# The closing exponential in a tile of its own, and the opening of the feed-forward part shared out anew

## The chip, the cores and the metric

The kernel runs on one core of a Trainium2 chip. The metric is the device time of one execution in microseconds (us); three executions gave 2990.84, 2991.1 and 2994.2 us, median 2991.1. A core has five engines that work through instruction queues of their own, in order: TensorE (PE in the profile; its weight loads are PEld), VectorE (DVE), ScalarE (ACT), GpSimd (POOL) and SyncE (SP), which here only issues DMAs. Engines wait for each other through semaphores.

## The reference

4096 nodes with 256 features and a 4096 x 4096 adjacency matrix go through two layers. Each layer adds a graph part and a feed-forward part to the running x:

```python
x = x + gnn0(layernorm(x), adj)     # 4 heads of 64, softmax over the neighbours, elu
x = x + ffn0(layernorm(x))          # 30 times: h + .01 tanh(h); h*sigmoid(h); layernorm; h @ W.T + b
x = x + gnn1(layernorm(x), adj)     # two graph layers, one after the other
x = x + ffn1(layernorm(x))          # router, the best 2 of 6 experts
```

A graph layer computes, for each head, scores `leaky_relu(f1[i] + f2[j])` where there is an edge, a softmax over j, the weighted sum of the values and `elu` of the result. So there are three graph layers in all: g0, g1 and g2.

## The kernel before, in words

Rows are taken in tiles of 128 and groups of four tiles (512 rows; 8 groups). The kernel has six stages in order: graph layer g0, the feed-forward part of 30 steps, g1, g2, and the experts (routing and products).

**A graph layer** (`attention`) begins with a prologue that multiplies the rows by the weights (`columns` transposes a group and writes the tile xT, L276; `products` multiplies, L302). Its main loop has 128 units, in the order of chunk c (8 row tiles, 4 chunks), head h (4) and column block q (8). In a unit ScalarE or VectorE makes signs (L461, L459), VectorE masks them (L569, L575), and TensorE adds up products in the PSUM tiles acc (L521). The exponentials are split so that no exponential is needed per edge. The queues of VectorE and ScalarE are in the order of the code here (`manual_schedule`).

When the 8 units of a head are through, it is closed while the next head's first units run. `lower_sums` (ScalarE, L468) and `whole_sums` (VectorE, L472) take acc out into the tile u, which frees acc for the next head. Then `close` takes one step a unit: scale (L482), add (L486), add and reciprocal (L489, L491), divide (L495), exponential on ScalarE (L499), and `finish` (L625 or L627, then L628), which makes elu of it and adds the old x. `finish` ends with the store to DRAM (L629, on SP's queue). There is one buffer for u, and the exponential e is written into a free half of it:

```python
e = u[:, :, 1, :D]
nc.scalar.activation(e[:, :nt], o[:, :nt], AF.Exp)
```

L628 writes its result over e, so the store reads u. Adjacency masks come from DRAM in pieces of 1 MB (`load_mask`, L192) in g1 and g2, four for each chunk, during the chunk's last head before; they go through SP's queue too. The last head of a layer is closed after the loop (L603 to L608), outside the written order: a planner merges its steps among the instructions of the next stage by its own estimate of times.

Memory is given out in pools, stacked in the order in which they are opened and freed as a stack. The prologue's pools (prep, pw) and the closing pool (end) of a layer start at the same address, since the one pair is freed before the other is opened.

**The feed-forward part** works on units, one group in one step: 240 units. A unit passes through a pipeline over slots (`slot`): slot `at` does tanh of unit `at` on ScalarE (L881) and adds it to the input on GpSimd (L882); Silu (L869) and its f16 copy (L871) of unit at-2 on ScalarE, the rest of that split (L872) and the statistics (L896, L898) on VectorE, and a transposing DMA (L876, SP); the transposes of unit at-3 on TensorE (L845), their copy on ScalarE (L903), the standard deviation (L906 to L908); the matmuls of unit at-4 (L920, L923); and the scaling of unit at-5 (L853). The queues of TensorE, VectorE, ScalarE and GpSimd are in written order in this part. A manual dependency makes GpSimd's sum of unit `at` wait for L872 of unit at-2; in the very first slot it waits for `closed[0]`, the division L495 of the last close.

Its input must be normalised first, group by group: `measure` (VectorE, 4 x L748 and 4 x L750), `rate` (one small instruction on ScalarE, L756, three on GpSimd, L757 to L760), `init` (four ScalarE instructions, L766). Groups 0 to 3 are loaded into the tile ring and measured beside the last units of g0, by a table `side` that is keyed by units left (L788); groups 4 to 7 are handled in the first slots (L909 to L914). Groups 6 and 7 hold the rows of g0's last chunk, so their loads (L822) wait for the store of the last close.

The weights of the three graph layers (`weights`, L128) lie in the pool keep from the start of the kernel, though those of g2 are only loaded during g1 (L977).

Of the kernel before, what the change touches and what calls it, by code (L numbers as in the profile page):

```python
# [11 lines left out]
F32 = mybir.dt.float32  # L12
# [5 lines left out]
AF = mybir.ActivationFunctionType  # L18
# [28 lines left out]
def gnn_ffn_kernel(ctx: ExitStack, tc: tile.TileContext, a: dict, out: bass.AP):  # L47
# [79 lines left out]

    def weights(tag, W, a_src, a_dst, norm):  # L128


        w = keep.tile([P, KC, C + 2 * H], F32, name=f"{tag}_w")

# [28 lines left out]
    def attention(tag, src, norm, w, front, chunks, first, ends, following, side={}):  # L161
# [7 lines left out]
        with ExitStack() as scope:  # L169
# [306 lines left out]
            def close(c, h, u):  # L476

                nt, t0 = chunks[c], starts[c]
                begin, finish = ends
                more = begin(t0, nt, h, end)  # L480
                v = u[:, :, 0, :]
                nc.vector.tensor_tensor(  # L482
                    v[:, :nt], v[:, :nt], r[:, t0 : t0 + nt, h : h + 1].to_broadcast([P, nt, DV]), OP.mult
                )
                yield
                nc.vector.tensor_tensor(v[:, :nt], v[:, :nt], u[:, :nt, 1, :], OP.add)  # L486
                yield

                nc.vector.tensor_tensor(v[:, :nt], v[:, :nt], hs[:, :, h, :].to_broadcast([P, nt, DV]), OP.add)  # L489
                z = end.tile([P, CM, 1], F32, name="z", bufs=2)  # L490
                nc.vector.reciprocal(z[:, :nt], v[:, :nt, D : D + 1])  # L491
                yield
                o = v[:, :, :D]
                closed[:] = [
                    nc.vector.tensor_tensor(o[:, :nt], v[:, :nt, :D], z[:, :nt].to_broadcast([P, nt, D]), OP.mult)  # L495
                ]
                yield
                e = u[:, :, 1, :D]
                nc.scalar.activation(e[:, :nt], o[:, :nt], AF.Exp)  # L499
                yield  # L500
                finish(t0, nt, h, o[:, :nt], e[:, :nt], more)
                yield
# [107 lines left out]
    def to_rows(dst, src=None):  # L610
# [12 lines left out]
        def finish(t, n, h, u, e, old):  # L623
            if src is None:
                nc.vector.tensor_scalar(u, u, 0.0, -1.0, op0=OP.max, op1=OP.add)  # L625
            else:
                nc.vector.scalar_tensor_tensor(u, u, 0.0, old, op0=OP.max, op1=OP.add)  # L627
            nc.vector.scalar_tensor_tensor(e, e, 1.0, u, op0=OP.min, op1=OP.add)  # L628
            nc.sync.dma_start(block(dst, t, n, h), e)  # L629

        return begin, finish


    layers = [weights("g0", a["L0_gnn_W"], a["L0_gnn_a1"], a["L0_gnn_a2"], True)]
    for n in range(2):
        av = a[f"L1_gnn_a{n + 1}"]
        layers.append(weights(f"g{n + 1}", a[f"L1_gnn_W{n + 1}"], av[:, :D], av[:, D:], not n))
    gw = [w for w, _ in layers]
    w0 = gw[0]

# [121 lines left out]

    def init(g):
        rs, nm = rates.pop(g)
        for r in range(G):
            nc.scalar.activation(  # L766
                x1[g][:, r, :], x1[g][:, r, :], AF.Identity, scale=rs[:, r : r + 1], bias=nm[:, r : r + 1]
            )

# [5 lines left out]
    def front(prep, small_ps):  # L775
# [17 lines left out]
        20: [(load, 3)],  # L793
        14: [(measure, 0)],
        8: [(measure, 1)],
        4: [(rate, 0), (rate, 1), (measure, 2)],
        1: [(measure, 3), (init, 0), (init, 1), (rate, 2), (rate, 3)],
# [14 lines left out]
    with ExitStack() as scope:  # L812
# [18 lines left out]
        th, zs, mvs, rs, zT, zT16, pos = {}, {}, {}, {}, {}, {}, {}  # L831
        units = FFN_STEPS * NG
        def slot(at):
            g, part = divmod(at - 4 * NG, 3 * NG)
# [32 lines left out]
            if 0 <= u < units:  # L867
                z = zs[u] = work.tile([P, G, C], F32, name="z")
                nc.scalar.activation(z, th.pop(u), AF.Silu, scale=0.01)  # L869
                z16 = work.tile([P, 2, G, P], F16, name="z16", bufs=4)  # L870
# [6 lines left out]
            if at < units:  # L877
# [3 lines left out]
                nc.scalar.activation(th[at], was, AF.Tanh, scale=0.01)  # L881
                ins = nc.gpsimd.tensor_tensor(th[at], th[at], was, OP.add)  # L882
                if not at:
                    lower = closed[0]
                if lower is not None:
                    tc.add_manual_dep(
                        ins.ins,
                        lower.ins.name,
                        mybir.DependencyInfo(mybir.DependencyClass.Sync, mybir.DependencyReason.DATA),
                        reason="the port that both use",  # L890
                    )
            if 0 <= u < units:
# [8 lines left out]
            if 0 <= u < units:  # L901
# [6 lines left out]
                nc.gpsimd.tensor_tensor(rs[u], rs[u], under[:, int(u >= units - NG), :], OP.mult)  # L908
            if 4 <= at + 3 < NG:  # L909
                rate(at + 3)  # L910
            if 2 <= at + 2 < NG:
                init(at + 2)
            if 4 <= at + 4 < NG:
                measure(at + 4)  # L914
            u = at - 4
# [19 lines left out]
        with tc.manual_schedule(  # L935
# [5 lines left out]
            }  # L941
        ):
            for at in range(units):
                slot(at)
# [25 lines left out]


    def centre_weights(prep, small_ps):
        layers[1][1][2](small_ps)
# [5 lines left out]
    for n in range(2):  # L979
# [3 lines left out]
            not n,  # L983
            gw[n + 1],
            None if n else centre_weights,
# [463 lines left out]
```

## Time and profile before

One execution was profiled. Engines' busy times are of that one.

| | |
|---|---|
| median of three runs | 2991.1 us |
| the profiled execution | 2996.19 us |
| its span, first to last instruction | 2994.5 us |
| granted TensorE clock, mean | 0.975 |
| busy: TensorE, VectorE, ScalarE, GpSimd | 2805.8, 2735.7, 2472.4, 1160.0 us |
| g0's last matmul ends | about 602.3 us |
| first, last tanh of the feed-forward part (start) | 602.9, 1547.0 us |
| g1's last, g2's first large matmul | about 2116.9, 2128.1 us |
| g2's last sums begin (L472) | 2674.0 us |

In a line of groups the columns are: line, engine, operation, written tile <- read tiles, shapes, count; busy us and mean ns of one; then the engine's idle us just before and what ended most of it. In a timeline line they are: start, duration, engine, line, operation, tiles, shapes, count, and in brackets the idle time before it with what ended it. SPq is SP's queue of DMA issues.

### The profile page before, as it was taken

What the parts mean: (1) busy time and instruction counts of PE and PEld (TensorE: products, weight loads), DVE (VectorE), ACT (ScalarE), POOL (GpSimd) and SP (SyncE); (2) the same over time, 40 slices, a digit from 0 to 9 for tenths busy, and PEclk for the clock granted to TensorE, in tenths of its full rate; (3) what the DMA queues carried; (4) which work ended last, traced back from release to release, by engine and by line L of the source; (5) the groups of instructions that cost most, each with busy time, mean ns of one, the idle gap of its engine ahead of it and who ended that gap; (6) DMA issues with size and microseconds to landing.
All of it is one profiled execution on the core that took longest, in us unless ns stands there. A gap on an engine that the chain in (4) does not pass through costs nothing. (4 is left out here: it accounts for less than half of the span.)

```text
span 2994.5 us, 82658 instructions
## 1 busy us (share of the span) xinstructions
PE 2805.8 (94%) x33923; PEld 2567.1 (86%) x33923; DVE 2735.7 (91%) x5756; ACT 2472.4 (83%) x3137; POOL 1160.0 (39%) x1085
## 2 busy tenths in 40 slices
PE   7899999979999999999998999999789999986996
PEld 6799999958888888888887999999689999985996
DVE  7999999989999999999998899999689989986775
ACT  6799999888888888888877999999689989963342
POOL 3000000089999999999982000000200000014663
PEclk9999999989999999999999999999999999997998
DMA  9998785053333333433352122120302132123253
GB/s 287 276 255 249 221 245 144 23 127 69 69 70 68 68 68 68 68 68 68 69 119 101 31 93 85 36 90 24 107 22 91 52 106 79 52 85 137 80 172 136
DMA packets 484451, 320.08 MB, mean 107 GB/s; under 512 B 416589, under 2 KB 445418, under 8 KB 477930
## 3 DMA queue, kind: packets, MB, share of 16 engines
q1 hardware_dynamic: 474034, 290.27, 37.2%
q0 software_dynamic: 7104, 19.41, 2.0%
q8 instruction: 268, 4.39, 0.6%
q10 hardware_dynamic: 2936, 5.11, 0.5%
q14 instruction: 109, 0.89, 0.1%
HBM read 183.00 MB, written 52.04 MB: 78 GB/s over the span
## 5 line engine op out<-in xcount | busy, mean ns | idle before, releaser
L521 PE MATMUL acc<-vals,st 128*128 128x130 f16 x12288 | 1435.2, 219 | 44.5 <-DVE u L472 37.2
L521 PE MATMUL acc<-vals,below 128*128 128x130 f16 x12288 | 1434.9, 221 | 12.0 <-DVE below L575 11.4
L461 ACT ACTIVATE st<-f1b,nf 128x1024 int8<-128x1024 f32 x1265 | 1335.7, 1142 | 38.0 <-PE acc L521 24.0
L521 PEld LDWEIGHTS <-below 128*128 128x128 fp8e4 x12288 | 1178.0, 96 | 58.8 <-issue 53.4
L521 PEld LDWEIGHTS <-st 128*128 128x128 fp8e4 x12288 | 1209.5, 98 | 8.9 <-DVE st L569 6.9
L920 PE MATMUL po<-wT,zT 128*128 128x256 f32 x1920 | 575.0, 381 | 3.7 <-ACT zT L903 3.7
L923 PE MATMUL po<-w,zT 128*128 128x256 f16 x3840 | 577.0, 273 | 1.3 <-DMA zT<-z 1.3
L882 POOL TENSOR_TENSOR th<-th,y 128x1024 f32<-128x1024 f32 x232 | 548.5, 2364 | 14.8 <-issue 0.2
L923 PEld LDWEIGHTS <-zT 128*128 128x128 f16 x3840 | 376.0, 98 | 161.8 <-DMA zT<-z 2.0
L575 DVE TENSOR_TENSOR below<-m,st 128x1024 int32<-128x1024 int32 x384 | 470.0, 1224 | 32.9 <-DVE st L569 1.4
L569 DVE TENSOR_TENSOR st<-st,m 128x1024 int32<-128x1024 int32 x384 | 467.3, 1217 | 0.2
L853 DVE SCALAR_TENSOR_TENSOR y<-po,z_rs,bias 128x256 f32<-128x256 f32 x928 | 384.6, 477 | 1.7 <-PE tp L845 0.4
L896 DVE BATCH_NORM_STATS2 z_st<-z 128x6 f32<-128x256 f32 x960 | 335.9, 413 | 0.0
L920 PEld LDWEIGHTS po<-wT,zT 128*128 128x128 f32 x1920 | 290.6, 191 | 12.8 <-ACT zT L903 4.5
L869 ACT ACTIVATE z<-th 128x1024 f32<-128x1024 f32 x240 | 251.8, 1049 | 14.6 <-POOL th L882 14.4
L106 POOL TENSOR_TENSOR ln_rstd<-ln_rstd,mhalf 128x4 f32<-128x4 f32 x24 | 31.1, 1296 | 583.9 <-ACT acc L1102 497.9
L907 POOL TENSOR_TENSOR z_rs<-z_rs,mhalf 128x4 f32<-128x4 f32 x240 | 244.5, 1019 | 3.1 <-ACT z_rs L906 3.1
L881 ACT ACTIVATE th<-y 128x1024 f32<-128x1024 f32 x232 | 241.7, 1042 | 0.0
L903 ACT COPY zT<-tp 128x512 f32<-128x512 f32 x240 | 140.4, 585 | 91.8 <-PE tp L845 90.4
L459 DVE TENSOR_SCALAR st<-f1b,nf 128x1024 int8<-128x1024 f32 x271 | 201.2, 743 | 8.1 <-PE acc L521 8.1
L757 POOL TENSOR_TENSOR x_rs<-x_rs,mhalf 128x4 f32<-128x4 f32 x8 | 10.2, 1280 | 505.4 <-ACT x_rs L756 505.4
L436 POOL MEMSET hs<- 128x4 f32 x3 | 0.3, 102 | 494.5 <-DVE u L489 494.5
(260 smaller groups left out, 3142.3 us busy)
## 6 DMA issues: line engine op xcount, KB each, us to landing
ring<-in_adj_dram SPq DMA_DIRECT2D x64, 1024.0 KB
m<-edges SPq DMA_DIRECT2D x32, 1024.0 KB
f1b<-fd SPq DMA_DIRECT2D x48, 512.0 KB
edges<-m SPq DMA_DIRECT2D x16, 1024.0 KB
y<-yd SPq DMA_DIRECT2D x16, 512.0 KB
ew<-in_L_ffn_expert_w_dram SPq DMA_DIRECT2D x18, 256.0 KB
t<-in_x_dram SPq DMA_DIRECT2D x8, 512.0 KB
old<-in_x_dram SPq DMA_DIRECT2D x16, 256.0 KB
```

The lines of the kernel that those rows point to most:

```text
L461: nc.scalar.activation(out, f1, AF.Sign, bias=f2, scale=-1.0)
L521: nc.tensor.matmul(acc[:, i, cols], masked[part][:, at_i // TR, s, rows], v[:, cols], start=(j == 0 and part == 0), stop=(j == NT - 1 and ...
L569: nc.vector.tensor_tensor(above, above, whole, OP.bitwise_and)
L575: nc.vector.tensor_tensor(below, whole, above, OP.bitwise_xor)
L853: nc.vector.scalar_tensor_tensor(t[:, r, :] if end else y[:, g * G + r, :], po[:, r, :], rstd[:, r : r + 1], t[:, r, :] if end else bias, ...
L869: nc.scalar.activation(z, th.pop(u), AF.Silu, scale=0.01)
L881: nc.scalar.activation(th[at], was, AF.Tanh, scale=0.01)
L882: ins = nc.gpsimd.tensor_tensor(th[at], th[at], was, OP.add)
L896: nc.vector.bn_stats(st[:, r, :], z[:, r, :])
L907: nc.gpsimd.tensor_tensor(rs[u], rs[u], mhalf, OP.pow)
L920: nc.tensor.matmul(po[:, r, :], src[:, r * P : (r + 1) * P], wT, start=True, stop=False)
L923: nc.tensor.matmul(po[:, r, :], src16[:, part * G + r, :], w16[:, other, :], start=False, stop=(part == 1 and other == 1),)
```

## The change

It has five parts.

1. In `close`, e is a tile of its own in the pool end (2048 bytes a partition, one buffer). `closed` now holds two instructions of the last close: what `finish` returns (its last VectorE instruction, L628 of before), and the exponential.
2. To make room, g2's weights move from keep to a pool "late" that is opened after the feed-forward part.
3. The first sum of the feed-forward part (unit 0) is VectorE's; GpSimd's first is unit 1, and it waits for `closed[0]`, now the end of the close.
4. Groups 3, 4 and 5 are initialised by VectorE (one `tensor_scalar` a tile, after `closed[0]`). What the first slots do for groups 2 to 7 is a table, `opening`: groups 4 and 5 are measured ahead of slot 0, both their rates are in slot 1, the measuring of groups 6 and 7 moves from slots 2 and 3 to 3 and 4, and the rest by one or two slots. In `side`, measuring 0 and 1 move from 14 and 8 units before the end to 18 and 14, the rates of both from 4 to 10.
5. The first Silu waits for the close's exponential.

```diff
-    def weights(tag, W, a_src, a_dst, norm):
+    def weights(tag, W, a_src, a_dst, pool):
-        w = keep.tile([P, KC, C + 2 * H], F32, name=f"{tag}_w")
+        w = pool.tile([P, KC, C + 2 * H], F32, name=f"{tag}_w")
...
-                closed[:] = [
-                    nc.vector.tensor_tensor(o[:, :nt], v[:, :nt, :D], z[:, :nt].to_broadcast([P, nt, D]), OP.mult)
-                ]
+                nc.vector.tensor_tensor(o[:, :nt], v[:, :nt, :D], z[:, :nt].to_broadcast([P, nt, D]), OP.mult)
                 yield
-                e = u[:, :, 1, :D]
-                nc.scalar.activation(e[:, :nt], o[:, :nt], AF.Exp)
+                e = end.tile([P, CM, D], F32, name="e")
+                powers = nc.scalar.activation(e[:, :nt], o[:, :nt], AF.Exp)
                 yield
-                finish(t0, nt, h, o[:, :nt], e[:, :nt], more)
+                closed[:] = [finish(t0, nt, h, o[:, :nt], e[:, :nt], more), powers]
...
-            nc.vector.scalar_tensor_tensor(e, e, 1.0, u, op0=OP.min, op1=OP.add)
+            made = nc.vector.scalar_tensor_tensor(e, e, 1.0, u, op0=OP.min, op1=OP.add)
             nc.sync.dma_start(block(dst, t, n, h), e)
+            return made
...
+    def follows(ins, other, reason):
+        tc.add_manual_dep(
+            ins.ins,
+            other.ins.name,
+            mybir.DependencyInfo(mybir.DependencyClass.Sync, mybir.DependencyReason.DATA),
+            reason=reason,
+        )
-    def init(g):
+    def init(g, apart=False):
         rs, nm = rates.pop(g)
         for r in range(G):
-            nc.scalar.activation(
-                x1[g][:, r, :], x1[g][:, r, :], AF.Identity, scale=rs[:, r : r + 1], bias=nm[:, r : r + 1]
-            )
+            t = x1[g][:, r, :]
+            if apart:
+                ins = nc.vector.tensor_scalar(t, t, rs[:, r : r + 1], nm[:, r : r + 1], op0=OP.mult, op1=OP.add)
+                follows(ins, closed[0], "first the rows that others wait for")
+            else:
+                nc.scalar.activation(t, t, AF.Identity, scale=rs[:, r : r + 1], bias=nm[:, r : r + 1])
...
-        14: [(measure, 0)],
-        8: [(measure, 1)],
-        4: [(rate, 0), (rate, 1), (measure, 2)],
+        18: [(measure, 0)],
+        14: [(measure, 1)],
+        10: [(rate, 0), (rate, 1)],
+        4: [(measure, 2)],
...
+        opening = {
+            0: [(init, 2)],
+            1: [(rate, 4), (rate, 5), (init, 3, True)],
+            2: [(init, 4, True)],
+            3: [(init, 5, True), (measure, 6)],
+            4: [(rate, 6), (measure, 7)],
+            5: [(init, 6), (rate, 7)],
+            6: [(init, 7)],
+        }
...
-                nc.scalar.activation(z, th.pop(u), AF.Silu, scale=0.01)
+                ins = nc.scalar.activation(z, th.pop(u), AF.Silu, scale=0.01)
+                if not u:
+                    follows(ins, closed[1], "one change of tables")
...
-                ins = nc.gpsimd.tensor_tensor(th[at], th[at], was, OP.add)
-                if not at:
+                ins = (nc.gpsimd if at else nc.vector).tensor_tensor(th[at], th[at], was, OP.add)
+                if at == 1:
                     lower = closed[0]
...
-            if 4 <= at + 3 < NG:
-                rate(at + 3)
-            if 2 <= at + 2 < NG:
-                init(at + 2)
-            if 4 <= at + 4 < NG:
-                measure(at + 4)
+            for f, g, *how in opening.get(at, []):
+                f(g, *how)
...
+            measure(4)
+            measure(5)
             for at in range(units):
                 slot(at)
...
+    layer(2, ctx.enter_context(tc.tile_pool(name="late", bufs=1)))
```

More of the change, by code (lines that the diff above doesn't have):

```diff
@@ L627, in finish, with layer @@
                 nc.vector.scalar_tensor_tensor(u, u, 0.0, old, op0=OP.max, op1=OP.add)
-            nc.vector.scalar_tensor_tensor(e, e, 1.0, u, op0=OP.min, op1=OP.add)
+            made = nc.vector.scalar_tensor_tensor(e, e, 1.0, u, op0=OP.min, op1=OP.add)
             nc.sync.dma_start(block(dst, t, n, h), e)
+            return made
         return begin, finish
[L634 to L639, printed above, removed]
+    layers = [weights("g0", a["L0_gnn_W"], a["L0_gnn_a1"], a["L0_gnn_a2"], keep)]
+    w0 = layers[0][0]
+    def layer(n, pool):
+        av = a[f"L1_gnn_a{n}"]
+        layers.append(weights(f"g{n}", a[f"L1_gnn_W{n}"], av[:, :D], av[:, D:], pool))
+    layer(1, keep)
     def begin_weights(n):
@@ L881, in slot @@
                 nc.scalar.activation(th[at], was, AF.Tanh, scale=0.01)
-                ins = nc.gpsimd.tensor_tensor(th[at], th[at], was, OP.add)
-                if not at:
+                ins = (nc.gpsimd if at else nc.vector).tensor_tensor(th[at], th[at], was, OP.add)
+                if at == 1:
                     lower = closed[0]
                 if lower is not None:
[L886 to L891, printed above, removed]
+                    follows(ins, lower, "the port that both use")
             if 0 <= u < units:
@@ L983, in gnn_ffn_kernel @@
             not n,
-            gw[n + 1],
+            layers[n + 1][0],
             None if n else centre_weights,
```

## The prediction

> **What bounds the kernel now.** I read the page first: TensorE and VectorE are both busy for over nine tenths, so what matters is where TensorE stands still.
>
> ```profile
> span 2994.5 us, 82658 instructions
> PE 2805.8 (94%) x33923; PEld 2567.1 (86%) x33923; DVE 2735.7 (91%) x5756; ACT 2472.4 (83%) x3137; POOL 1160.0 (39%) x1085
> L521 PE MATMUL acc<-vals,st 128*128 128x130 f16 x12288 | 1435.2, 219 | 44.5 <-DVE u L472 37.2
> ```
>
> 37.2 of the 44.5 us that the attention's matmuls idle end with L472, the first step of a head's close: it empties the accumulators. The VectorE groups, with shapes kept apart, say what L472 itself waits for:
>
> ```profile
> L472 DVE TENSOR_TENSOR u<-acc,lo 128x520 f32<-128x520 f32 x96 | 66.9, 697 | 54.4 <-ACT lo L468 35.2 <-DMA h1d<-u 10.9 <-DMA x3d<-u 6.2
> ```
>
> 17.1 us are waits for the *store of the head before*, which reads u, the tile that L472 overwrites; its line's own view adds 1.7 us for x1d. The timelines (VectorE, then SP's queue, then TensorE) at the worst place, in the second graph layer:
>
> ```profile
> 2422.94 0.69 DVE L628 SCALAR_TENSOR_TENSOR u<-u 128x512 f32<-128x512 f32 x1
> 2430.71 0.70 DVE L472 TENSOR_TENSOR u<-acc,lo 128x520 f32<-128x520 f32 x1 [3.28 <-DMA x3d<-u]
> ...
> 2422.33 0.32 SPq L192 DMA_DIRECT2D m<-edges  x1
> 2423.66 0.46 SPq L629 DMA_DIRECT2D x3d<-u  x1
> ...
> 2431.46 0.27 PE L521 MATMUL acc<-vals,st 128*128 128x130 f16 x1 [2.39 <-DVE u L472]
> ```
>
> The store follows a 1 MB mask load and needs 7 us; all engines then stand. The same views between the two graph layers:
>
> ```profile
> 2127.40 0.60 ACT L276 ACTIVATE xT<-tp 128x512 f32<-128x512 f32 x1 [5.34 <-DMA h1d<-u]
> ...
> 2123.28 0.37 SPq L629 DMA_DIRECT2D h1d<-u  x1
> ...
> 2128.14 6.85 PE L302 MATMUL ph<-g_w,xT 128*128 128x264 f32 x16 [8.77 <-ACT xT L276]
> ```
>
> The next layer's xT lies in u's memory, so ScalarE waits for the last store. Last, the opening of the feed-forward part (ScalarE, VectorE, GpSimd, TensorE):
>
> ```profile
> 608.02 2.06 ACT L766 ACTIVATE ring<-ring,x_nm,x_rs 128x256 f32<-128x256 f32 x4
> 610.09 1.28 ACT L869 ACT_TABLE_LOAD   x1
> 611.39 1.06 ACT L869 ACTIVATE z<-th 128x1024 f32<-128x1024 f32 x1
> 616.82 1.04 ACT L869 ACTIVATE z<-th 128x1024 f32<-128x1024 f32 x1
> ...
> 608.15 2.42 DVE L627 SCALAR_TENSOR_TENSOR u<-u,old 128x512 f32<-128x512 f32 x1 [0.70 <-ACT u L499]
> 610.60 2.72 DVE L628 SCALAR_TENSOR_TENSOR u<-u 128x512 f32<-128x512 f32 x1
> ...
> 607.67 5.10 POOL L882 TENSOR_TENSOR th<-th,ring 128x1024 f32<-128x1024 f32 x2 [5.68 <-DVE u L495]
> ...
> 612.50 1.11 PE L845 MATMUL tp<-ident,z 128*128 128x128 f32 x4 [10.18 <-ACT z L869]
> ```
>
> TensorE is idle for 10.18 us and again for 4.30; ScalarE carries row groups (2.06 us each, L766) between the Silus, and the last close's L627 and L628 take 2.42 and 2.72 us beside GpSimd's sums. From 642.3 us TensorE runs without a gap, 3.92 us a unit; only what it starts earlier there counts.
>
> **The Trainium skill.** "SBUF — State Buffer", section "Who interferes with whom": a VectorE operation with two SBUF inputs and a GpSimd operation that reads SBUF exclude each other for a whole instruction. The trace agrees: 2.42 and 2.72 us there, 0.69 where GpSimd is idle. "DMA: Bandwidth & Descriptors", section "Latency and other measured facts": latency at HBM is 0.2 us, but 2 us under high load. Agrees in kind: stores landed after 2.8 us (613.35 to the load freed at 616.19), 4.1, 5.5 and 7 us, the longest behind mask loads. "ScalarE: Activation LUTs", section "What ACT_TABLE_LOAD costs": 1283 ns, and 1380 more for a drain; the trace shows the first and no gap for the second, so I use 1.3.
>
> **Part 1, the exponential's own tile.** The store reads e, so u is free once VectorE itself has read it (L628, in order before L472). The new wait sits on the next Exp, which overwrites e five units after L472: 19 us later, against a store of 7, so nothing. What the stalls cost TensorE I take from the cadence of L468, the ScalarE copy that starts with the end of a head's matmuls. Undisturbed: 29.97 to 30.0 us. After the closes with a store wait: 30.89, 29.97, 30.72 in layer one; 30.38, 33.53 (2427.26 to 2460.80), 30.79 in layer two. Over 29.98: 0.91+0+0.74+0.40+3.55+0.81 = **6.4 us**. Masks do not become late next: the one needed at such a close was loaded six units before. The fourth wait of layer one (5.49 us at 2116.54) gives nothing: the second L472 waits there for L468, which ends at 2117.49 anyway.
>
> In layer zero 1.11 and 0.57 us of VectorE idling end with x1d. VectorE is the bound there (572 of 600 us busy), so most of it comes back: **1.5** (0 to 1.7).
>
> Between the graph layers: prep and work pools of a layer start where the attention's closing pool starts. By the sizes in the code u is bytes 0 to 4160, two lo to 8320, z to 8384, and the new e 8384 to 10432. The next layer's small tiles and first xT (2272 to 6368) lie under u and lo, the second xT (6368 to 10464) under e. So the first xT waits for L628 (2123.25), not the landing (2127.40): **4.1 us**. The second xT, at 2136.15 before, moves to about 2132, after the landing. If e were laid first, this would be 0.
>
> **Part 2, the opening.** I walk the in-order queues with the trace's durations; walked in the old order, they start the f16 part of unit 4's matmuls at 643.25, where the trace has 643.21. New: L495 ends at 607.44 as before. The first sum runs on VectorE, priced by L370 (same shape, 1.22 us), while Exp runs; L627 and L628 take 0.69 each and end at 610.0 (before 613.3). ScalarE has no third group between Exp and the table load: Silu 0 at 609.4 (611.39). VectorE's groups 3 to 5 wait for L628 on their own queue, which costs nothing; L872 of unit 0 is behind group 3, but its port is taken until 612.5 anyway. GpSimd's first sum, unit 1, waits for L628 instead of following L495; behind it queue the rates of groups 4 and 5 (1.56 each). It runs 610.1 to 612.5, Silu 1 at 612.5 (616.82). Then the gain shrinks: the sum of unit 2 queues behind both rates, Silu 2 at 618.0 (624.00); group 6's measuring on VectorE comes after two groups of 4 x 0.325 and the Silus' statistics (1.6 us a unit), so rate 6 on ScalarE, ahead of Silu 3, holds that to 623.4 (630.21); group 6's initialisation on ScalarE waits for its rate, behind unit 4's sum on GpSimd, so Silu 4 is at 631.4 (635.49). Unit 4's matmuls get to the same point at 640.4, 2.8 earlier.
>
> The two unknowns: how VectorE's tensor_scalar behaves beside GpSimd (L1092, same shape, mean 452 ns with GpSimd near, 1.38 us for four without; if it waits out each sum, gain 1.95), and whether the planner puts the first sum before L482 (0.8 less). Together **2.3 us**, ends 1.2 and 2.85. ScalarE is relieved of 3 x 2.06 = 6.2 us; were all of it on the path, that is the upper bound. One change of tables stays one: the old order has only one there; its new wait (Silu 0 behind Exp) is met at 608.1, and what queues behind Silu 0 on ScalarE is late only if Exp is.
>
> SP's queue: the store of the last close is issued at 610.1 instead of 613.35, so the two loads behind it (L822) and unit 0's transposing DMA behind them come some 3 us earlier; the walk has that. Ring reloads behind the first sum wait for VectorE's instead, about 1 us earlier.
>
> **Part 3, nothing.** Measuring 1 (1.6 us) moves off the close at 571.88, where TensorE idled 2.31, but measuring 0 moves ahead of the close at 539.43; VectorE has no idle between, so the loss only changes place. If VectorE had cover at 532, this would gain 1.6. The moved measurings and rates issue no DMA; earlier rates use idle GpSimd. Layer two's weights swap one place in memory for another; nobody waits for them.
>
> **Sum.** 6.4 + 1.5 + 4.1 + 2.3 = 14.3. Profiled: 2994.5 to 2980.2 span. That execution took 2996.19 us, 5 over the median 2991.1; I apply the sum to the median: **2977**. A measurement can tell about 0.2%, 6 us.
>
> **Rivals.** (a) Half of it: xT is not freed (the layout differs) or the opening gives nothing since its rates queue behind the sums: 2980 to 2983. For: the walk already loses most of the 6.2 us. Against: the sizes above. (b) The opening gives all 6.2 and the measuring 1.6: 2991.1 - 6.4 - 1.5 - 4.1 - 6.2 - 1.6 = 2971. Against: GpSimd's rates. (c) Store waits belong to the profiled run, and stores land earlier without it: then 6.4+1.5+4.1 shrink to perhaps 3 and it ends at 2986 to 2990, no change. For: that run is 5 us longer. Against: 1 MB mask loads ahead of the stores are no matter of profiling. (d) Slower: a unit is 3.92 us on TensorE while VectorE is busy 19.97 of 20 us in steady units and GpSimd 19.2. If the new phase of VectorE against GpSimd makes L872 meet a running sum in each of some 235 units, the unit grows; from 0.06 us a unit it eats all 14.3, at 0.1 the time is 2991.1 - 14.3 + 23.5 = 3000. Against: each sum waits for L872 two units back, which restores the old phase.
>
> **Numbers.** My case 55%, (a) 20%, (b) 8%, (c) 10%, (d) 7%. My case alone: 2973 to 2981. Range with (a) and (b): 2971 to 2986. Faster by over 0.2% are mine, (a), (b): 0.83; same 0.10; slower 0.07.
>
> **What would show it.** L472 with no DMA among its releasers; heads of 30.0 us throughout both graph layers; first xT after the last store's issue, not its landing; L627 and L628 at 0.69 us; Silu 1 near 612.5 from the same start; first gapless unit 2 to 3 us earlier; 3.92 us a unit as before. Wrong, if a new wait for e appears at Exp, if TensorE's idle at L472 stays at 37 us, or if steady units lengthen.

## The result, and the profile after

The changed kernel takes 2985.93 us (median of twelve executions, 2983.95 to 2989.26); the kernel before, on the same chip, 2992.97 us (twelve, 2989.34 to 2996.2). The ratio is 0.9978, with a 95% interval of 0.9969 to 0.9987: 7.0 us faster. The direction was forecast; of the 14.3 us of the sum, half came.

The two profiled executions lie further apart, 2994.5 and 2982.6 us of span. The one of before took 2996.19 us, no less than the slowest of its twelve (2996.2); the one of after 2984.29 us, the second fastest of its twelve. A part of those 11.9 us is no work of the change; the experiments say which.

The page of the changed kernel, its span, engines, and the group of attention matmuls that was shown of before:

```profile
span 2982.6 us, 82658 instructions
PE 2801.3 (94%) x33923; PEld 2561.3 (86%) x33923; DVE 2740.8 (92%) x5769; ACT 2465.6 (83%) x3125; POOL 1153.7 (39%) x1084
L519 PE MATMUL acc<-vals,st 128*128 128x130 f16 x12288 | 1430.7, 218 | 37.7 <-DVE u L472 30.2
```

The same matmuls idle 37.7 us where they idled 44.5, all of the difference at L472. The groups with shapes kept apart say what L472 itself waits for now:

```profile
L472 DVE TENSOR_TENSOR u<-acc,lo 128x520 f32<-128x520 f32 x96 | 66.8, 696 | 44.7 <-ACT lo L468 44.4
```

No store is left among its releasers. At the place in g2 where everything stood for a store before, the timelines of VectorE, SP's queue and TensorE now read:

```profile
2415.54 0.69 DVE L626 SCALAR_TENSOR_TENSOR e<-e,u 128x512 f32<-128x512 f32 x1
2423.07 0.70 DVE L472 TENSOR_TENSOR u<-acc,lo 128x520 f32<-128x520 f32 x1 [0.74 <-ACT lo L468]
...
2414.93 0.32 SPq L192 DMA_DIRECT2D m<-edges  x1
2416.26 0.37 SPq L627 DMA_DIRECT2D x3d<-e  x1
...
2423.82 0.22 PE L519 MATMUL acc<-vals,st 128*128 128x130 f16 x1 [0.30 <-DVE u L472]
```

The store still follows a 1 MB mask load, but L472 no longer waits for it; TensorE stands 0.30 us instead of 2.39. Between the graph layers, though (ScalarE, SP's queue, VectorE, TensorE):

```profile
2121.69 0.60 ACT L276 ACTIVATE xT<-tp 128x512 f32<-128x512 f32 x1 [5.31 <-DMA h1d<-e]
...
2117.60 0.37 SPq L627 DMA_DIRECT2D h1d<-e  x1
...
2116.88 0.69 DVE L626 SCALAR_TENSOR_TENSOR e<-e,u 128x512 f32<-128x512 f32 x1
...
2122.43 5.99 PE L302 MATMUL ph<-g_w,xT 128*128 128x264 f32 x16 [8.73 <-ACT xT L276]
```

ScalarE still waits 5.31 us for the last store (5.34 before). And in the opening of the feed-forward part (ScalarE, VectorE, GpSimd, TensorE):

```profile
605.07 1.28 ACT L891 ACT_TABLE_LOAD   x1
606.36 1.06 ACT L891 ACTIVATE z<-th 128x1024 f32<-128x1024 f32 x1
609.27 1.06 ACT L891 ACTIVATE z<-th 128x1024 f32<-128x1024 f32 x1
621.48 0.30 ACT L757 ACTIVATE x_rs<-x_mv,eps 128x4 f32<-128x4 f32 x1 [2.91 <-DVE x_mv L751]
...
605.81 0.69 DVE L626 SCALAR_TENSOR_TENSOR e<-e,u 128x512 f32<-128x512 f32 x1
606.61 3.42 DVE L777 TENSOR_SCALAR ring<-ring,x_rs,x_nm 128x256 f32<-128x256 f32 x4
612.21 3.38 DVE L777 TENSOR_SCALAR x<-x,x_rs,x_nm 128x256 f32<-128x256 f32 x4
617.76 2.10 DVE L777 TENSOR_SCALAR x<-x,x_rs,x_nm 128x256 f32<-128x256 f32 x4
...
606.73 2.51 POOL L906 TENSOR_TENSOR th<-th,ring 128x1024 f32<-128x1024 f32 x1 [8.80 <-DVE e L626]
612.65 2.47 POOL L906 TENSOR_TENSOR th<-th,ring 128x1024 f32<-128x1024 f32 x1
...
626.94 0.67 PE L935 MATMUL po<-wT,zT 128*128 128x256 f32 x2 [3.24 <-DVE y L875]
```

The close ends with 0.69 us instructions and the first Silus come early, as forecast. But the three row groups that VectorE took over (L777) need 3.42, 3.38 and 2.10 us, where four such instructions alone need about 1.4 (the 1.38 of the prediction): in each group one instruction runs into a GpSimd sum and ends 0.15 us after it. VectorE is late, so rate 6 waits 2.91 us for its measuring and TensorE 3.24 us for a scaling, L875.

Heads are a clock for the comparison: L468, the ScalarE copy at the end of a head's matmuls, comes in two parts for each head, and the start of the first is counted (48 heads, from 1). The table gives the time between such starts for all profiled executions, those of the experiments too. "Feed-forward" is the step from head 16 to head 17, "transition" from 32 to 33, "rest" from head 48 to the end of the span (the expectations count this one as head 47).

| profiled execution | heads 1 to 16 (g0) | feed-forward | 17 to 32 (g1) | transition | 33 to 48 (g2) | rest |
|---|---|---|---|---|---|---|
| before | 474.6 | 1061.16 | 453.37 | 101.94 | 454.51 | 323.0 |
| after | 471.0 | 1061.35 | 451.57 | 100.65 | 449.65 | 322.9 |
| own_tile | 474.4 | 1061.79 | 451.57 | 99.12 | 449.67 | 338.3 |
| opening_only | 472.7 | 1060.95 | 453.81 | 101.41 | 452.44 | 338.9 |
| early_pool | 473.9 | 1060.95 | 451.58 | 94.84 | 449.67 | 351.1 |
| scalar_inits | 473.9 | 1060.00 | 451.59 | 101.33 | 449.66 | 336.7 |
| early_g1 | 472.5 | 1061.38 | 451.58 | 95.38 | 449.66 | 336.4 |
| after_again | 471.3 | 1060.77 | 451.62 | 100.17 | 449.70 | 335.5 |
| imm | 472.9 | 1061.14 | 451.61 | 99.46 | 449.69 | 337.5 |
| best | 472.4 | 1105.50 | 451.62 | 96.30 | 449.71 | 335.6 |
| both | 471.0 | 1060.15 | 451.57 | 97.93 | 449.66 | 334.6 |
| both2 | 471.0 | 1060.03 | 451.56 | 95.74 | 449.67 | 335.8 |
| both2, timed | 473.9 | 1059.92 | 451.59 | 95.61 | 449.67 | 322.0 |
| slip | 474.0 | 1101.14 | 451.57 | 99.12 | 449.67 | 335.3 |

The runs were on several chips; the rest of the kernel took 12 to 16 us longer on some of them, which is why only times beside the kernel before on the same chip, or stretches, are compared.

Between before and after, g1 and g2 gave 1.80 and 4.86 us, together 6.7; the transition 1.3; the feed-forward part nothing (-0.2). The 3.6 us of g0 are largely no gain of the change: slip has the changed kernel's g0, instruction for instruction, and took 474.0, after_again 471.3.

For the opening there is a sharper mark than that step: the start of the f16 part of unit 4's matmuls, where the prediction's walk ended (before, then after):

```profile
643.21 0.60 PE L923 MATMUL po<-w,zT 128*128 128x256 f16 x4
...
639.11 0.60 PE L938 MATMUL po<-w,zT 128*128 128x256 f16 x4
```

Counted from head 16's L468 (600.51 and 596.45), that is 42.71 us before and 42.66 after. In every execution but those of best and slip, 923.7 us lie between it and the part's last f16 matmul, so this start is what the opening is worth. The opening gained 0.05 us.

### The profile page after: what moved, and what is told of

Read it like the earlier page. It is cut to its first block, busy times and chain, and to the rows that moved or that the text cites. A ratio compares the mean times of both kernels' runs of the same rounds, so it can differ in the third digit from the quotient of the medians.

```text
span 2982.6 us, 82658 instructions
## 1 busy us (share of the span) xinstructions
PE 2801.3 (94%) x33923; PEld 2561.3 (86%) x33923; DVE 2740.8 (92%) x5769; ACT 2465.6 (83%) x3125; POOL 1153.7 (39%) x1084
## 5 line engine op out<-in xcount | busy, mean ns | idle before, releaser
L519 PE MATMUL acc<-vals,st 128*128 128x130 f16 x12288 | 1430.7, 218 | 37.7 <-DVE u L472 30.2
L875 DVE SCALAR_TENSOR_TENSOR y<-po,z_rs,bias 128x256 f32<-128x256 f32 x928 | 384.3, 476 | 2.2 <-PE tp L867 0.7
L926 POOL TENSOR_TENSOR z_rs<-z_rs,mhalf 128x4 f32<-128x4 f32 x240 | 245.0, 1021 | 3.1 <-ACT z_rs L925 3.1
```

The lines of the kernel that those rows point to most:

```text
L519: nc.tensor.matmul(acc[:, i, cols], masked[part][:, at_i // TR, s, rows], v[:, cols], start=(j == 0 and part == 0), stop=(j == NT - 1 and ...
L875: nc.vector.scalar_tensor_tensor(t[:, r, :] if end else y[:, g * G + r, :], po[:, r, :], rstd[:, r : r + 1], t[:, r, :] if end else bias, ...
L926: nc.gpsimd.tensor_tensor(rs[u], rs[u], mhalf, OP.pow)
```

## The experiments

The theory from this profile: the gain is the store waits in the heads; the transition kept its wait because a new pool waits for the pool whose place it takes, as a whole; the opening gave nothing because the row groups on VectorE are shut out by GpSimd's sums. Rivals: the opening carries a part of the gain; what follows in the transition is bound by something else; GpSimd's rates and sums, not VectorE, bind the opening.

### own_tile: the exponential's tile alone

```diff
 (the kernel before)
-                e = u[:, :, 1, :D]
+                e = end.tile([P, CM, D], F32, name="e")
...
+    layer(2, ctx.enter_context(tc.tile_pool(name="late", bufs=1)))
```

> The kernel before, with the exponential in its own tile and the third layer's weights laid late, and nothing of the new opening. My theory: this alone is the whole gain, so 6 to 8 us under before (ratio about 0.9977): heads of layers one and two at 29.96 us throughout, the step from head 32 to head 33 at about 100.7 us (101.94 before), the first heads of layer zero shorter by some 2 to 4 us together. Rival, the opening carries a part of it: only 3 to 5 us under before (0.9985 to 0.999).

3005.89 us beside 3011.55 of before: ratio 0.9982 (0.9975 to 0.9989), 5.7 us in the medians and 5.4 by the ratio. g1 and g2 have the lengths of the changed kernel to 0.02 us. These are medians of executions without a profile, so the store waits are no matter of the profiled execution alone. The size lies just under the 6 to 8 us expected, and the interval overlaps widely with the changed kernel's (0.9969 to 0.9987): most of the gain, perhaps all of it. The step from head 32 to 33 took 99.12 us rather than 100.7. One part of the expectation failed: g0 took 474.4 us, not 2 to 4 less than the 474.6 of before.

### opening_only: everything but the tile

```diff
 (the changed kernel)
-                e = end.tile([P, CM, D], F32, name="e")
+                e = u[:, :, 1, :D]
```

> The changed kernel with the exponential back in u's half; the opening and the moved measurings stay. My theory: no gain, 0 +- 1 us (ratio 0.9997 to 1.0003), and from the last matmul of layer zero to the first head of layer one 1061 to 1061.5 us as in both kernels. Rival, the opening is worth its forecast 2.3 us: ratio 0.9992 and 1059 us there.

Ratio 1.0004 (0.9995 to 1.0013), 1060.95 us from layer zero to one. No gain that can be measured. Its heads also size the store waits a second time: g1 and g2 took 2.24 and 2.77 us longer than with the tile, together 5.0, where the profile of before had 6.7. The worst head took 31.64 us here, 33.54 there, with the same instructions in both. The wait is real in both; how long it is differs from execution to execution.

### early_pool and early_g1: what holds the first xT

In early_pool the exponential's tile of every layer lies in a pool opened ahead of the steps, so that nothing of the next layer is laid at its address; in early_g1 only that of g1.

```diff
 (the changed kernel; early_g1. early_pool without the condition)
+            own = scope.enter_context(tc.tile_pool(name=f"{tag}_own", bufs=1)) if tag == "g1" else None
...
-                e = end.tile([P, CM, D], F32, name="e")
+                e = (own or end).tile([P, CM, D], F32, name="e")
```

> The changed kernel with the exponential's tile in a pool of its own that is opened ahead of the steps, and so outlives the pools of the preparation at that address: nothing of the next layer takes its place. Theory, the first xT waited for the store because the new pool waits for all tiles of the pool whose place it takes: the first xT of the third layer is now released by L626 on VectorE, 3 to 4 us after which the whole rest comes earlier; the step from head 32 to 33 takes 97 to 98 us instead of 100.65, and the time is 3 to 4 us under the changed kernel (ratio to before about 0.9966). Rival, what follows is bound by something else (the second row group's load, the products' copies): the step stays at 100 us or more and the ratio at 0.9977.

The transition fell to 94.84 us, but the ratio is 0.9986 (0.9979 to 0.9993), no better than the changed kernel. The profile has the loss in the rest: 351.1 us from head 48 on, 12 to 14 more than its three neighbours on that chip. The planner, which orders the steps outside the written queues by its own estimates, had put the experts' first instructions in another order: TensorE's matmuls stand in another order from the 32,148th of 33,923 on, at the start of the experts. So the comparison was not clean, and early_g1 makes it clean: every engine's instructions stand in the order of the changed kernel.

> The changed kernel with the exponential's tile of the second graph layer alone in a pool opened ahead of the steps; every engine's instructions then stand in the same order as in the changed kernel. Theory: the step from head 32 to head 33 takes 95 us (100.65 in the changed kernel), what comes after is unchanged (from head 47 to the end as long as in the changed kernel on this chip), and the time is 4 to 6 us under the changed kernel, ratio to before 0.996. Rival, the expert part takes it back with its old order too: the step at 95 us and the ratio at 0.998 or above.

ScalarE, SP's queue and VectorE at the transition in early_g1:

```profile
2119.12 0.60 ACT L276 ACTIVATE xT<-tp 128x512 f32<-128x512 f32 x1 [1.30 <-DVE e L626]
...
2119.03 0.37 SPq L627 DMA_DIRECT2D h1d<-e  x1
...
2118.31 0.69 DVE L626 SCALAR_TENSOR_TENSOR e<-e,u 128x512 f32<-128x512 f32 x1
```

The first xT now starts as the store is issued, 0.81 us after the start of L626 where the changed kernel needed 4.81. The transition takes 95.38 us beside 100.17 in after_again, the rest 336.4 beside 335.5. Ratio to before 0.9946 (0.9926 to 0.9966), beside 0.9964 for the changed kernel in the same series: 4.3 us in the medians, inside the 4 to 6 expected. In both kernels the first xT lies clear of e by its address (e at bytes 179,488 to 181,536 of a partition, first xT 173,376 to 177,472 in the changed kernel). That the wait is for more than the tile's own bytes is therefore shown. How far it reaches is not: the second buffer of the same new pool does lie under e (177,472 to 181,568), so the wait may be for all of the displaced pool, or only for what the new pool as a whole covers.

Over all profiled executions the first xT starts 12.1 to 12.5 us after head 32's L468 in the eight with g1's e in u or in the closing pool, and 8.3 us after it in the six with e in an early pool. The transition averages 99.98 us in the six with e in the closing pool and 95.97 in those six, 4.0 us apart; 4.1 were forecast for an xT that doesn't wait for the store.

### after_again: the changed kernel beside the others

> The changed kernel once more, beside the others on their chip: 6 to 8 us under before (ratio 0.9977), heads of layers one and two at 29.96 us, step from head 32 to 33 at 100.5 us, last matmul of layer zero to the first head of layer one 1060.9 to 1061.4 us. If the gain hung on one chip: ratio above 0.999.

2997.03 us beside 3006.82: ratio 0.9964 (0.9951 to 0.9976), a gain again, on another chip, of 9.8 us in the medians; the two intervals overlap between 0.9969 and 0.9976. The three stretches named in the expectation came within 0.4 us.

### scalar_inits: the row groups back on ScalarE

```diff
 (the changed kernel)
-            1: [(rate, 4), (rate, 5), (init, 3, True)],
-            2: [(init, 4, True)],
-            3: [(init, 5, True), (measure, 6)],
+            1: [(rate, 4), (rate, 5), (init, 3)],
+            2: [(init, 4)],
+            3: [(init, 5), (measure, 6)],
```

> The changed kernel with row groups 3 to 5 initialised by ScalarE again (2.06 us each), the rest of the new opening kept. Theory, the opening gave nothing since VectorE's form of the initialisation stands still beside GpSimd's sums (2.1 to 3.4 us a group instead of 1.3) and holds up measuring 6 and L875: VectorE gets 8.9 us back and the last matmul of layer zero to the first head of layer one takes 1.5 to 2.5 us less than the 1061.35 of the changed kernel. Rival, GpSimd's sums and rates carry the chain, or ScalarE's 6.2 us come back on the path: the same 1061.35 or up to 2 us more.

Counted from the last L468 of g0, Silu 1 comes 3.4 us later than in early_pool, which has VectorE's row groups (616.68 - 600.44 beside 613.75 - 600.94), but Silu 4 1.5 us earlier (632.49 and 634.51, less the same starts), and the feed-forward step takes 1060.00 us, 0.95 less than in opening_only and early_pool on the same chip. That is under the 1.5 to 2.5 expected, with the expected sign. The step also holds the way to g1's first head, which differs by 0.6 us between these executions; unit 4's f16 matmuls, free of that, start 41.13 us after head 16's L468, beside 42.63 to 42.68 in all six executions with the row groups normalised on VectorE, and 41.02 to 41.10 in those of both and both2. So the row groups on VectorE cost about 1.6 us more than on ScalarE. The ratio of 0.9968 (0.9956 to 0.9981) is of six executions and does not stand apart from the changed kernel's.

### imm: is it the two columns of scalars?

```diff
 (the changed kernel)
-                ins = nc.vector.tensor_scalar(t, t, rs[:, r : r + 1], nm[:, r : r + 1], op0=OP.mult, op1=OP.add)
+                ins = nc.vector.tensor_scalar(t, t, 1.0, 0.0, op0=OP.mult, op1=OP.add)
```

> The changed kernel with VectorE's row groups 3 to 5 multiplied by the constant 1 and added the constant 0 in place of the two columns of scalars: the normalisation of these rows is left out, the same elements are read and written, and the instructions wait for the same rates. If the columns of scalars are what shuts the instruction out while GpSimd runs a sum[...]: 0.2 to 0.42 us each, beside GpSimd too, and 1.3 us a group or less. If any VectorE instruction of this kind is shut out: single ones of 2.4 us as in the changed kernel.

One execution, in which these rows stay unnormalised. The line's own view of L777 gives the shortest, middle and longest duration in ns. In the changed kernel:

```profile
L777 DVE TENSOR_SCALAR x<-x,x_rs,x_nm x8: 378/405/2433, 612.2 to 619.5; 128x256 f32<-128x256 f32 x8
L777 DVE TENSOR_SCALAR ring<-ring,x_rs,x_nm x4: 400/408/2447, 606.6 to 609.6; 128x256 f32<-128x256 f32 x4
```

and in imm:

```profile
L777 DVE TENSOR_SCALAR x<-x x8: 256/282/1123, 614.1 to 620.6; 128x256 f32<-128x256 f32 x8
L777 DVE TENSOR_SCALAR ring<-ring x4: 281/288/2452, 608.8 to 611.6; 128x256 f32<-128x256 f32 x4
```

With constants the instruction is shorter (282 to 288 ns instead of 405), but it is shut out all the same: 2452 ns beside a sum. The columns of scalars are not the cause. That no form of tensor_scalar escapes is more than two forms can show. The second group met no sum in imm (0.86 us for the four, 3.38 in the changed kernel), the three together took 5.66 us instead of 8.90, and unit 4's matmuls start at 41.84 us: VectorE's time is on the path.

### best, both, both2: putting the gains together

best is early_g1 with the row groups on ScalarE, and measurings 6 and 7 with rates 6 and 7 moved a unit ahead (the expectation names rate 6 alone, the kernel moves both):

```diff
 (early_g1; the new lines of the table alone)
+            1: [(rate, 4), (rate, 5), (init, 3)],
+            2: [(init, 4), (measure, 6)],
+            3: [(rate, 6), (init, 5), (measure, 7)],
+            4: [(rate, 7)],
+            5: [(init, 6)],
```

> The second layer's tile as in early_g1, row groups 3 to 5 back on ScalarE, and measurings 6 and 7 and rate 6 each one unit earlier, VectorE standing idle at both places. Theory: 4 to 6 us at the step from head 32 to 33, 1 us from the row groups, and up to 1.4 us from ScalarE's wait for rate 6, so from the last head of layer zero to the first of layer one 1058.6 to 1059.5 us and a ratio to before of 0.9950 to 0.9955. Rival, TensorE starts at half speed after its idle and takes back what starts earlier: 1060 us there.

3039.94 us, ratio 1.0110 (1.0088 to 1.0132): 33 us slower than before; neither case of the expectation came. The loss is in the feed-forward part, 1105.50 us. From 900 to 1300 us GpSimd begins 97 units where it begins 103 in early_g1, and its power L926 takes 1.47 us a unit instead of 1.02, VectorE's L896 0.97 instead of 0.74 (medians). Its opening is the best of all, with unit 4's matmuls at 39.75 us, and is lost more than tenfold in the units after it. This is the slower rival of the forecast, (d), met in a kernel of my own. both leaves measurings and rates where the changed kernel has them; both2 moves measuring 6 and rate 6 alone.

> early_g1 and scalar_inits together, nothing else: the second layer's exponential in the early pool, row groups 3 to 5 on ScalarE, measurings and rates where the changed kernel has them. Theory: both gains, 4.5 us at the step from head 32 to 33 (95 to 95.5 us) and 1 us from the last head of layer zero to the first of layer one (1060 us), so 12 to 15 us under before (ratio 0.995 to 0.996) and 5 to 6 under the changed kernel. Rival, the feed-forward part falls into the longer unit of the run best: 3040 us.

2993.5 us beside 3006.41, ratio 0.9953 (0.9937 to 0.9969); feed-forward 1060.15, transition 97.93 us. The feed-forward part has its short unit; the transition gained less than expected. The first xT is as early as in early_g1 (8.32 us); 1.3 us are lost before the first unit of g2, where TensorE waits 1.29 us for a ScalarE copy (L322), as it does in opening_only and scalar_inits too, and 1.3 after it. What makes these come and go is open.

> The run before, both, with measuring 6 and rate 6 one unit earlier as in best, measuring 7 and rate 7 left. It tells which move of best lengthens the unit. Theory, a single late moment of GpSimd puts the steady part into the longer unit, where L896 meets the power L926 in place of L927: with one rate less moved ahead of the sums it stays at 3.92 us a unit and 1058.6 to 1060 us between the layers. Rival, measuring 6 ahead of L896 of unit 1 is enough: 1105 us and L926 at 1.47 us.

1060.03 and 95.74 us. So measuring 6 ahead is harmless, and the further moves of best (measuring 7 and rate 7 a unit ahead) tip it over. It gains nothing either: unit 4's matmuls start at 41.02 us, since group 7's initialisation on ScalarE waits 1.19 us for its rate, a wait that best does not have. Timed:

> The kernel both2 timed beside the kernel before. Theory: 12 to 16 us under before, ratio 0.9950 (0.993 to 0.996), the feed-forward part at 1060 us and the step from head 32 to 33 at 95 to 98 us as in its one look. If the earlier measuring is on the edge of the longer unit, single executions at 3030 us or more.

2980.73 us (2979.25 to 2983.32) beside 2991.74: ratio 0.9964 (0.9950 to 0.9978), 11 us, with no execution in the long unit. By these intervals early_g1, both and both2 beat the kernel before, as the changed kernel does, and their intervals overlap with the changed kernel's; what sets them apart are the stretches, 4.0 us on average in the transition and 1.6 us in the opening.

### slip: can one late moment lengthen every unit after it?

```diff
 (the changed kernel, feed-forward slot)
+            if at == 60:
+                idle = small.tile([P, G], F32, name="idle", bufs=1)
+                for _ in range(3):
+                    nc.gpsimd.tensor_tensor(idle, under[:, 0, :], mhalf, OP.pow)
```

> The changed kernel with three more powers of 128 x 4 (1.02 us each) on GpSimd at unit 60 of the feed-forward part, and nothing else there. Theory, two steady states: pushed late once, GpSimd meets L896 with its power (L926 1.47 us, L896 0.97 us) and needs 4.02 us a unit, more than TensorE's 3.92, so it never comes back: from unit 60 on the longer unit, 25 to 40 us more between the layers (1086 to 1101 us). Rival, the waits between VectorE and GpSimd restore the old phase: 1061.4 to 1064.5 us.

1101.14 us in one execution, 40 more than in the changed kernel, from 3.17 us of work once: the upper end of what was expected. GpSimd's and VectorE's timelines around it:

```profile
849.21 1.03 POOL L926 TENSOR_TENSOR z_rs<-z_rs,mhalf 128x4 f32<-128x4 f32 x1
850.32 0.41 POOL L927 TENSOR_TENSOR z_rs<-z_rs,under 128x4 f32<-128x4 f32 x1
850.69 3.17 POOL L933 TENSOR_TENSOR idle<-under,mhalf 128x4 f32<-128x4 f32 x3
853.83 2.35 POOL L906 TENSOR_TENSOR th<-th,y 128x1024 f32<-128x1024 f32 x1
856.13 1.47 POOL L926 TENSOR_TENSOR z_rs<-z_rs,mhalf 128x4 f32<-128x4 f32 x1
857.68 0.20 POOL L927 TENSOR_TENSOR z_rs<-z_rs,under 128x4 f32<-128x4 f32 x1
...
849.93 0.74 DVE L896 SCALAR_TENSOR_TENSOR z<-z,scale,z 128x512 f16<-128x512 f32 x1
854.20 2.52 DVE L896 SCALAR_TENSOR_TENSOR z<-z,scale,z 128x512 f16<-128x512 f32 x1
859.79 0.95 DVE L896 SCALAR_TENSOR_TENSOR z<-z,scale,z 128x512 f16<-128x512 f32 x1
```

Until 850 us L896 falls on the small L927, which then takes 0.41 us instead of 0.20, and GpSimd's unit is 2.37 + 1.02 + 0.41 = 3.80 us, under TensorE's 3.92. Once GpSimd is late, L896 has to wait out a whole sum (2.52 us), and from then on it starts at the end of a sum and falls on the power: 2.36 + 1.47 + 0.20 = 4.03 us, over TensorE's 3.92. GpSimd is then the bound and never comes back; 97 units in 400 us are 4.12 us each, with GpSimd's other additions, and 180 units of 0.20 us more and the slip itself make 39 us. The rival, that the waits restore the old phase, has fallen. In best the same rhythm begins in the opening: L926 takes 1.49 us at 626.90 us and 1.47 from then on, and GpSimd runs on from 618.96 us, where in both2 it stands idle for 1.24 us before 635.45 and L926 takes 1.02. That this idle time is what saves both2 is likely, not shown.

## Why the prediction was right or wrong

**The store waits (6.4): right in mechanism and place.** L472 has no store among its releasers; the six heads after a store took 29.96 us each, and no new wait came up at the exponential (its ScalarE group idles 5.9 us in all, every bit on VectorE's L494). g1 and g2 gave 6.7 us in the profiled pair, 5.0 between opening_only and the runs beside it. The forecast size was read from one execution, and that one was on the long side.

**g0's 1.5: not settled, and small.** Executions of the same g0 code differ by 3 us (471.0 to 474.0), more than the term. The second step between heads took 34.08 and 33.74 us with e in u, and 31.7 in all twelve executions with the tile; but the next took 31.7 with e in u and 32.7 to 34.3 with the tile, so little or nothing of it stays. Part 3 is nothing, as forecast: g0's last three steps take 92.5 us before and after. (In the first 600 us the trace has VectorE busy for 565, not the 572 that the prediction read.)

**The transition (4.1): the step that failed first.** "So the first xT waits for L628 (2123.25), not the landing (2127.40)" took the layout for the rule. The layout was as worked out, and the wait stayed: 5.31 us for the store, released by the landing. early_pool and early_g1 show it from the other side: with e in another pool the wait ends with L626, and the transition gives 4.0 us on average. So the size was right and the condition wrong: a tile of a new pool can wait for more than the bytes that it takes. The 1.3 us that the changed kernel gained here are not the store, since the first xT starts 12.36 us after head 32's L468 before and 12.32 after. 0.9 of them lie in the sixteen matmuls behind it, 6.85 and 5.99 us; the granted clock in these stretches was 0.55 and 0.64, and the next groups' sixteen took 4.60 to 3.73. Executions of the same code differ there as much (5.92 in after_again, 6.38 in slip), so this gain was chance.

**The opening (2.3, ends 1.2 and 2.85): the step that failed second.** The walk put unit 4's f16 matmuls at 640.4, 39.9 us after head 16's L468; they start at 42.66, before at 42.71. The forecast Silu 1 came near (12.82 us; the walk had 12.0, before 16.31), the gain was gone by unit 4. The term mis-sized is VectorE's row group: I priced it at 4 x 0.325 = 1.3 us and let the bad case cost no more than 0.35 us of the gain. It took 3.42, 3.38 and 2.10 us, some 4.8 us more in all than three undisturbed groups, and with measuring 6 and L875 behind it on VectorE's queue, 1.6 us of the gain went (scalar_inits, both and both2 at 41.0 to 41.1). Another 1.3 us came only when measuring 7 and rate 7 were a unit earlier too (best, 39.75): the walk followed group 6's rate and had no term for group 7's. The prediction's second unknown also came out badly: the planner put VectorE's first sum between L482 and L486, and the division ended 7.93 us after head 16's L468 instead of 6.93; what that cost at unit 4 no run takes apart.

The sign was in the line that the prediction read for this. L1092 of before has a mean of 452 ns, but most single ones take 0.40 us and a few 0.56 to 0.82 (VectorE, then GpSimd):

```profile
2692.02 2.14 DVE L1092 TENSOR_SCALAR n<-ring,ln_rstd,nmr 128x256 f32<-128x256 f32 x4
...
2692.04 0.65 POOL L1024 IOTA along_i<- 128x512 int32 x1
2692.75 0.61 POOL L1030 CAST along<-along_i 128x512 f16<-128x512 int32 x1
```

The first two of these four take 0.82 and 0.76 us, and each ends 0.15 us after one of GpSimd's short instructions. Beside a sum of 2.36 us such a wait is three times as long. The section of the Trainium skill that the prediction leaned on, "Who interferes with whom" in "SBUF — State Buffer", lists tensor_scalar among the operations that can take the shared port in their fast modes; I had taken only its sentence on two inputs. The traces here show the exclusion for one input, with constants and with columns (2.43 to 2.45 us beside a sum, 0.28 and 0.40 alone).

**The sum.** Without the two failed terms it is 6.4 + 1.5 = 7.9 us; 7.0 were measured, by the interval 4 to 9. That 2985.93 still falls inside the stated 2971 to 2986, at its very end, is no merit of the sum: the range had been stretched for (a).

**Rivals.** (a), half of it because xT is not freed or the opening gives nothing, is what happened, both halves of its "or" at once, but hardly for its reasons: the layout did not differ, and rates behind GpSimd's sums (group 7's in both2, 1.19 us) are only a part of what held the opening. The two halves together are why the result lies above (a)'s own 2980 to 2983. (1.9 us of that distance are the kernel before, whose median was 2991.1 in the runs that the forecast started from and 2992.97 beside the changed kernel.) (b) needed an opening of 6.2 us and did not come. (c) left 3 us for all waits together; own_tile's unprofiled executions gave 5.4 (3.3 to 7.5), so the waits are no misfortune of the profiled execution, but (c) was right about the size of the sum: it was made against one of the slowest executions and applied to a median. (d) did not befall this change: units stayed at 3.92 us. But my reason against it, that the manual dependencies restore the phase, was wrong, as slip shows; 3.17 us of GpSimd's time at the wrong moment would have cost this change all that it gained and 30 us more.

## What to carry to other kernels

A buffer that is free by its address need not be free for the program: where pools are stacked, ask what the displaced pool still waits for, and put the tile with the slow reader in another pool. Moving work from an engine with slack to one at its limit is paid at the price it has there, next to whatever else runs; look at the single instructions behind a mean before taking it for a price. And where two engines run in lockstep at 97% of the bound, look for the second rhythm that the same queues can fall into: take the worst overlap of each pair of instructions and ask if the unit then exceeds the bound.

## What the runs showed of the hardware

A VectorE tensor_scalar of 128x256 fp32 takes 0.28 us with constants and 0.40 us with two columns of scalars, and either one up to 2.45 us when GpSimd is in the midst of a 128x1024 addition; a batch-norm statistic that reads the same shape keeps its 0.41 us there (388 to 411 ns in 23 that ran wholly beside one, in the opening of the changed kernel). A store of 256 KB behind a mask load varies enough between executions of the same instructions to move a single head by nearly 2 us (33.54 and 31.64). After 8.7 us of idle time, TensorE's sixteen 128x264 matmuls took 6.85 and 5.99 us, at a granted clock of 0.55 and 0.64; the same sixteen a group later took 4.60, and 3.73 after that. A pipeline of in-order queues can have two steady rhythms, 3.92 and 4.12 us a unit here, and 3.17 us of late work picked one of them for the 700 us that followed.
